# Layer 1's strips: their new rows and partial sums loaded from ScalarE's queue, not from SP's

## The chip, the cores and the metric

One NeuronCore of a Trainium2 chip runs the whole kernel. The metric is the device time of one execution in microseconds (us); lower is better. Twelve runs of the kernel before have a median of 2482.11 us, the lowest 2476.35, the highest 2493.36.

## What is computed

A graph network of two layers over 3327 nodes (padded to 3328 = 26 blocks of 128) with 128 features. Layer 0 is a four-headed graph attention; layer 1, in which the change lies, is a graph convolution. Both have a norm in front and add to their input:

```
h = max(layernorm(x), 0)
x = x + L0(h, adj)            # attention, 4 heads, concatenated, times w
h = max(layernorm(x), 0)
x = x + L1(h, adj)
def L1(H, A, W, b):
    A_t = A + I;  D = A_t.sum(axis=1);  D_inv = D ** -0.5
    return relu((D_inv[:, None] * A_t * D_inv[None, :]) @ (H @ W.T + b))
```

About 2% of the adjacency matrix is not zero.

## The kernel before

**Layer 0** goes over the 26 blocks of nodes. For each it gathers rows of neighbours from a table in HBM, scores and weighs them, and closes the block (`close`): from the aggregate `agn` come the new rows `xn` of `x` (L786), stored to `xn_d` (L788, by SP), and from `xn` a row of the norm: `agn` again (L793, L794 on ScalarE), a transpose (L798 on TensorE), its copy (L799), a product with `gwT` (L806), `L809` on VectorE, and at last `x_sb[:, b]` (L811 on ScalarE). After that `x_sb[:, b]` holds what layer 1 multiplies for block b, already scaled.

**Layer 1** needs, for each row of the output, the sum over all 26 columns of blocks of `x_sb[:, j]` times the adjacency. The output is made in seven *strips* of four blocks (the last has two), transposed: `strips[s, j]` is a 128x512 tile of the turned adjacency, kept in HBM as `AT_d`. Much of these sums is done while layer 0 still runs: columns that were closed early are summed in `prep` and stored as `part1_d` (one partial sum per block, none for strip 0); for strips 1, 2 and 3 twelve columns more are summed by `begin` and stored as `part2_d`. What is left are 74 products of a column and a strip, in this order (`work`): strip 0 columns 0 to 24, strip 1 columns 14 to 24, then column 25 of strips 0 and 1, then strip 2 (18 to 25), strip 3 (22 to 25), strip 4 (14 to 25), strip 5 (18 to 25), strip 6 (22 to 25). Each product is L1006, in fp32 two matmul instructions on the page. Numbered 0 to 73, the strips end with products 36, 37, 45, 49, 61, 69 and 73.

The tiles for the products come in seven *pieces* of 11 products (the last of 8). `strip` (L911) loads a piece into one of four buffers `g`, by DMAs that alternate between SP's queue and GpSimd's (L915, L916). Piece 4 holds products 44 to 54, piece 5 products 55 to 65, piece 6 products 66 to 73. A buffer comes free when the last product of the piece four before has run: piece 6 takes the buffer of piece 2, so it waits for product 32.

A strip ends in two steps:

- `strip_in(s)` (L955) takes tiles `r0` (three buffers) and `r1` (two) and issues up to three loads: `xn_d` rows into `r0[:, 0]` (L961), `part1_d` into `r1[:, 0]` (L963, not for strip 0), `part2_d` into `r0[:, 1]` (L965, strips 1, 2 and 3). Each is 256 KB (128 KB for strip 6). It is called at the first product of strips 0 and 1, and for the others at the fifth product of the strip or at its last, whichever comes first (L1003).
- `strip_out(s)` (L968) is a generator that the loop advances once per product. It starts after the strip's last product: VectorE adds `part2` (L973) and `part1` (L975) to the sum (strip 0, with neither, is copied by ScalarE, L977). Two advances later TensorE transposes it (L982, four at a time), VectorE adds `x_sb`, multiplies by `dinv`, takes the maximum and adds the new rows (L983, L984, L985), and ScalarE's queue stores the result (L986).

**What sets the order.** The whole is written by hand under a manual schedule: each engine runs its instructions in the order in which the loop records them, and waits where it must. TensorE's queue therefore holds the transposes of strip s (L982) some products after its end, and nothing behind them runs until they have; ScalarE's queue holds the instructions of `close` for block 25 among all else. While the first 36 products run, `close` of block 25 is spread between them: in TensorE's order its transpose L798 stands after product 29, and product 36 is the first that needs block 25's `x_sb`.

**Waits of a DMA.** In the built program the DMAs of SP and of ScalarE together take turns, in the order in which they were recorded, on eight completion semaphores (DMAHW0 to DMAHW7). A DMA waits, on the engine that issues it, until the DMA that had the same semaphore before it has landed.

Of the kernel before, what the change touches and what calls it, by code (L numbers as in the profile page):

```python
# [15 lines left out]
P = 128  # L16
# [215 lines left out]
def _sparse_layers(tc, nc, x, adj, w1, w2, a, wlin, w, gw, gb, gb_sb, gwT, x_sb, dinv, flag, ident, out):  # L232
# [24 lines left out]
    with ExitStack() as l0:  # L257
# [4 lines left out]
        xn_d = dram.tile([NP, D], F32, name="xn_d")  # L262
        part1_d = dram.tile([D, NP], F32, name="part1_d")
        part2_d = dram.tile([D, NP], F32, name="part2_d")
# [80 lines left out]
        def finished(b):  # L345

            return max(0, 4 * (b // 4) - 2)
# [607 lines left out]
        def strip_in(s):  # L955

            n = min(4, NB - 4 * s)
            r0 = pr.tile([P, 2, BANK], F32, name="r0", bufs=3).rearrange("p k (b d) -> p k b d", b=4)[:, :, :n]
            r1 = pr.tile([P, 2, BANK], F32, name="r1").rearrange("p k (b d) -> p k b d", b=4)[:, :, :n]
            rows = slice(4 * s * P, (4 * s + n) * P)  # L960
            nc.sync.dma_start(r0[:, 0], xn_d[rows, :].rearrange("(b p) d -> p b d", p=P))  # L961
            if finished(4 * s):
                nc.sync.dma_start(r1[:, 0], part1_d[:, rows].rearrange("p (b i) -> p b i", b=n))  # L963
            if s in early:
                nc.sync.dma_start(r0[:, 1], part2_d[:, rows].rearrange("p (b i) -> p b i", b=n))  # L965
            return n, rows, r0, r1

        def strip_out(s, po, n, rows, r0, r1):  # L968
# [26 lines left out]
        def layer1():  # L995
            ending, sums, ins = [], {}, {}
            for i, (s, j) in enumerate(work):
                if i == in_front:
                    yield "all"
                w = min(4, NB - 4 * s) * P  # L1000
                if s not in sums:
                    sums[s] = ps_z.tile([P, 2, BANK], F32, name="z")[:, 0]
                if j == min(NB - 1, first_column(s) + 4 * (s not in front)):  # L1003
                    assert len(ending) < 2
                    ins[s] = strip_in(s)
                nc.tensor.matmul(sums[s][:, :w], x_sb[:, j, :], strips[s, j][:, :w], start=(j == first_column(s)), stop=(j == NB - 1))  # L1006
                if i % PIECE == PIECE - 1 or i == len(work) - 1:
                    allow("g")
                ending[:] = [f for f in ending if next(f, "end") != "end"]
                if j == NB - 1:  # L1010
                    ending.append(strip_out(s, sums.pop(s), *ins.pop(s)))
                yield "one"
            for e in ending:
                for _ in e:
                    pass
# [194 lines left out]
        with tc.manual_schedule():  # L1210
# [4 lines left out]
            n = len(groups)  # L1215
# [8 lines left out]
            for i in range(-1, n + 1):  # L1224
                if i + 1 < n:
                    slot()
                if 0 <= i < n:
                    b, hb, m = groups[i]
# [153 lines left out]
```

## Time and profile before

| | |
|---|---|
| median of 12 runs | 2482.11 us (2476.35 to 2493.36) |
| the profiled execution | 2481.43 us |
| its span, first to last instruction of the program | 2479.3 us |
| share of the span, busy: TensorE, VectorE, ScalarE, GpSimd | 90%, 83%, 26%, 71% |
| mean busy share of the DMA engines, up to the last two slices of 40 | 90% or more in each slice |
| last product and scores of layer 0 on TensorE (L657) | 2384.69 to 2385.40 |
| the 74 products of layer 1 (L1006) | 2385.33 to 2469.45 |
| strip endings on TensorE (L982), strips 0 to 6, start | 2425.13, 2438.17, 2447.43, 2451.59, 2462.39, 2468.42, 2471.59 |
| last L985 on VectorE | 2472.99 to 2473.41 |

Of 2479.3 us the last 95 are layer 1's products and strip endings; all that the change touches runs after 2386. In the tables of the trace, times are us from the start of the span. PE is TensorE, DVE VectorE, ACT ScalarE, POOL GpSimd, SP SyncE; a "q" behind the name is the engine's sequencer, which issues DMAs and waits. A row of the timeline gives start, duration, engine, line, operation, the tiles written and read, their shape and how many instructions were merged; in brackets the engine's idle time before it and what ended it.

### The profile page before, as it was taken

How to read it: one execution, taken by the hardware profiler on the slowest of the kernel's cores; microseconds unless marked ns; L12 is line 12 of the kernel's file. 1: busy time of each engine (PE TensorE's matmuls, PEld its weight loads, DVE VectorE, ACT ScalarE, POOL GpSimd, SP SyncE). 2: the span in 40 equal slices, each digit the busy share in tenths (PEclk: the TensorE clock that was granted, in tenths of full speed). 3: DMA queues.
4: the chain of work that ended last, by engine and by line, in shares of the span. 5: the costliest groups of instructions: out<-in, count | busy, mean ns of one | idle time of the engine just before them, and what ended most of it. 6: DMA issues, size and time to landing. Idle time of an engine off the chain costs nothing.

```text
span 2479.3 us, 51942 instructions
## 1 busy us (share of the span) xinstructions
PE 2223.3 (90%) x19254; PEld 1594.2 (64%) x19254; DVE 2053.6 (83%) x6426; ACT 639.7 (26%) x1547; POOL 1765.9 (71%) x1867
## 2 busy tenths in 40 slices
PE   6589889988988998999999999899999999999996
PEld 4456666666666666666676676666667667666653
DVE  7688988898898898889888888988988988896633
ACT  4122222223222222322222222232222222221110
POOL 3577777777777777777777777777777777777750
PEclk8699999999999999999999999999999999999998
DMA  9999999999999999999999999999999999999996
GB/s 302 375 352 328 351 329 317 352 354 325 323 368 333 326 358 345 326 334 364 327 329 349 344 315 347 349 321 329 360 325 323 355 343 318 338 335 330 366 306 174
DMA packets 401715, 826.93 MB, mean 334 GB/s; under 512 B 38435, under 2 KB 270383, under 8 KB 398127
## 3 DMA queue, kind: packets, MB, share of 16 engines
q0 software_dynamic: 144464, 628.85, 72.2%
q1 hardware_dynamic: 165343, 147.87, 18.9%
q10 hardware_dynamic: 91648, 46.80, 6.3%
q8 instruction: 155, 2.54, 0.4%
q14 instruction: 105, 0.86, 0.1%
HBM read 754.47 MB, written 113.22 MB: 350 GB/s over the span
## 4 chain that ended last, share of the span: by engine, by line
PE 40%; DVE 26%; DMA 17%; POOL 9%; issue 6%; SPq 1%; ACT 1%; DVEq 0%; POOLq 0%; ACTq 0%
DVE r L638 14%; PE z L622 14%; DMA g<-table,idx 13%; PE s L657 10%; POOL g L595 9%; DVE cand L422 3%; PE ag L670 2%; PE z L627 2%; DVE codes L410 2%; PE tr L379 1%; DVE cand L456 1%; DVE lists L453 1%; PE tr L942 1%; PE z L1006 1%; PE z L1124 1%
## 5 line engine op out<-in xcount | busy, mean ns | idle before, releaser
L595 POOL DMA_INDIRECT g<-table,idx x1664 | 1611.5, 968 | 576.7 <-issue 418.8
L638 DVE TENSOR_TENSOR r<-z,x1n 128x1024 f32<-128x1024 f32 x832 | 1010.8, 1215 | 130.7 <-PE z L622 128.2
L622 PE MATMUL z<-ident,g 128*128 128x128 f32 x6656 | 922.5, 278 | 107.8 <-DVE r L638 97.3
L622 PEld LDWEIGHTS z<-ident,g 128*128 128x128 f32 x6656 | 750.9, 142 | 245.2 <-DVE r L638 145.8
L657 PE MATMUL s<-r,sel 128*4 128x512 f32 (+1 forms) x3744 | 504.9, 579 | 9.9 <-DVE r L638 9.5
L698 ACT COPY ssb<-s 128x512 f32<-128x512 f32 x208 | 122.0, 586 | 495.5 <-PE s L657 495.0
L657 PEld LDWEIGHTS s<-r,sel 128*4 128x4 f32 x3744 | 86.1, 85 | 254.5 <-issue 179.8
L422 DVE MAX8 cand<-codes 128x8 f32<-128x52 uint16 x1664 | 217.7, 206 | 0.0
L670 PEld LDWEIGHTS ag<-g,wt 128*32 128x32 f32 x3328 | 117.7, 110 | 101.2 <-issue 93.8
L670 PE MATMUL ag<-g,wt 128*32 128x133 f32 x3328 | 159.4, 278 | 0.0
L633 DVE TENSOR_TENSOR r<-z,x1n 128x128 f32<-128x128 f32 x104 | 30.1, 289 | 151.4 <-PE z L627 149.0
L730 ACT ACTIVATE sc<-sc 128x32 f32<-128x32 f32 x208 | 47.9, 230 | 414.4 <-DVE sc L725 252.1
L367 ACT COPY at<-tr 128x512 f32<-128x512 f32 (+1 forms) x175 | 97.1, 555 | 215.0 <-PE tr L365 203.8
L453 DVE MAX8 lists<-cand 128x8 f32<-128x272 f32 (+1 forms) x338 | 133.2, 394 | 2.2
L365 PE MATMUL tr<-ident,adjb 128*128 128x128 f32 x676 | 109.1, 285 | 26.0 <-DMA adjb<-in_adj_dram 16.5
L635 ACT ACTIVATE r<-z 128x512 f32<-128x512 f32 x104 | 62.1, 597 | 258.0 <-DVE r L633 258.0
L709 PE MATMUL tr<-ident,ssb 128*128 128x128 f32 x832 | 124.9, 273 | 2.1 <-ACT ssb L698 2.1
L627 PE MATMUL z<-oi,x1b 128*128 128x256 f32 x416 | 125.2, 383 | 0.0
L595 POOL DMA_INDIRECT ge<-table,idxo x104 | 99.2, 953 | 32.9 <-issue 14.0
L456 DVE MATCH_REPLACE8 cand<-lists,cand 128x272 f32<-128x272 f32 (+1 forms) x312 | 118.0, 378 | 0.0
L410 DVE SCALAR_TENSOR_TENSOR codes<-adjb,code 128x832 uint16<-128x832 f32 x104 | 104.2, 1018 | 12.8 <-DMA adjb<-in_adj_dram 12.8
L622 PE MATMUL z<-ident,ge 128*128 128x128 f32 x416 | 83.1, 282 | 26.6 <-DVE r L638 26.6
(200 smaller groups left out, 2444.1 us busy)
## 6 DMA issues: line engine op xcount, KB each, us to landing
adjb<-in_adj_dram SPq DMA_DIRECT2D x26, 1664.0 KB
table<-AT_d SPq DMA_DIRECT2D x26, 1664.0 KB
AT_d<-at ACTq DMA_DIRECT2D x150, 256.0 KB
g<-table,idx POOLq DMA_INDIRECT x1664
table<-img SPq DMA_DIRECT2D x12, 1296.0 KB
adjb<-AT_d SPq DMA_DIRECT2D x72, 128.0 KB
g<-AT_d SPq DMA_DIRECT2D x25, 256.0 KB
g<-AT_d POOLq DMA_DIRECT2D x25, 256.0 KB
```

Of the source, the lines that this page charges most:

```text
L410: nc.vector.scalar_tensor_tensor(codes[:, i], adjb[:, c0:c0 + part], 0.0, code[:, c0:c0 + part], op0=OP.not_equal, op1=OP.mult, accum_out= ...
L422: nc.vector.max(cand[:, c, 8:].rearrange("p (r s) -> p r s", s=32)[:, :, sgm % 32], codes.rearrange("p a b -> p (a b)")[:, sgm % 32 * SEG: ...
L453: nc.vector.max(top, of)
L456: nc.vector.match_replace(out=of, in_to_replace=top, in_values=of, imm_value=0.0)
L595: return nc.gpsimd.indirect_dma_start(out=g[:, t, lo:hi], out_offset=None, in_=tab, in_offset=bass.IndirectOffsetOnAxis(ap=at[:, t:t + 1], ...
L622: nc.tensor.matmul(z[:, i, q * P:(q + 1) * P], g[:, m % 2 * 4 + q, c0:c0 + D], ident, is_transpose=True, start=(q == 0 or m < 8), stop=(m ...
L627: nc.tensor.matmul(z[:, i, :n], k.x1b[:, h * D:(h + 1) * D], k.oi[:, hb * n:(hb + 1) * n], start=False, stop=True, skip_group_check=True)
L638: nc.vector.tensor_tensor(r.rearrange("p h (i s) -> p h i s", s=16), z.rearrange("p h (i s) -> p h i s", s=16), k.x1n[:, 2 * hp:2 * hp + 2 ...
L657: nc.tensor.matmul(k.s[32 * h:32 * h + 4, :n], sel[:, h, 31 - row:35 - row], r[h // 2][:, h % 2, :n], start=(row == 0), stop=(last and (m ...
L670: nc.tensor.matmul(k.ag[32 * cg:32 * cg + 32, u, :WORK], wt[:, t].rearrange("p h q -> p (h q)"), g[:, t, f0:f0 + WORK], start=(w == 0 and ...
L698: nc.scalar.copy(ssb, s)
L709: nc.tensor.transpose(pt[:, q, :], ssb[:, q * P:(q + 1) * P], ident)
```

## The change

Three calls in `strip_in` go from SP's queue to ScalarE's; nothing else is changed.

```diff
-            nc.sync.dma_start(r0[:, 0], xn_d[rows, :].rearrange("(b p) d -> p b d", p=P))
+            nc.scalar.dma_start(r0[:, 0], xn_d[rows, :].rearrange("(b p) d -> p b d", p=P))
             if finished(4 * s):
-                nc.sync.dma_start(r1[:, 0], part1_d[:, rows].rearrange("p (b i) -> p b i", b=n))
+                nc.scalar.dma_start(r1[:, 0], part1_d[:, rows].rearrange("p (b i) -> p b i", b=n))
             if s in early:
-                nc.sync.dma_start(r0[:, 1], part2_d[:, rows].rearrange("p (b i) -> p b i", b=n))
+                nc.scalar.dma_start(r0[:, 1], part2_d[:, rows].rearrange("p (b i) -> p b i", b=n))
```

Seven strips issue 7 + 6 + 3 = 16 DMAs. In the built programs the instructions of TensorE, VectorE and GpSimd stand in the same order as before; SP has the 16 fewer and ScalarE the 16 more. On ScalarE they stand so (the waits are those of the built program after the change; DMA names its destination and source):

```
L698 TensorCopy ssb<-s 128x512 [waits PE_49]
L961 DMACopy r_29158<-xn_d 128x4x128 [waits DMAHW7_49]
L730 Activation sc<-sc 128x44 [waits DVE_49,Activation_49]
...
L774 TensorCopy outT<-tr 128x512 [waits DMAHW2_49,PE_49]
L961 DMACopy r_29292<-xn_d 128x4x128 [waits DMAHW6_49]
L963 DMACopy r_29293<-part_d 128x512 [waits DMAHW0_49]
L965 DMACopy r_29292<-part_d 128x512 [waits DMAHW3_49]
L793 Activation agn<-xn,st 128x128 [waits DVE_49,Activation_49]
...
L986 DMACopy out_dram<-r_29158 128x4x128 [waits DMAHW1_49,DVE_49]
L986 DMACopy out_dram<-r_29292 128x4x128 [waits DMAHW2_49,DVE_49]
L961 DMACopy r_29379<-xn_d 128x4x128 [waits DMAHW3_49]
L963 DMACopy r_29380<-part_d 128x512 [waits DMAHW4_49]
L965 DMACopy r_29379<-part_d 128x512 [waits DMAHW5_49]
L986 DMACopy out_dram<-r_29379 128x4x128 [waits DMAHW6_49,DVE_49]
L961 DMACopy r_29403<-xn_d 128x4x128 [waits DMAHW1_49,DMAHW7_49,PE_49,Activation_49]
```

From there on it goes on in the same way: the store of strip s, then the loads of strip s + 1 (loads of strips 2, 3, 4, 5 and 6 behind the stores of strips 1, 2, 3, 4 and 5).

## The prediction

> **What bounds the kernel now.** The change acts in the last 95 us alone, so I read that stretch: first the timeline of TensorE, VectorE and SP, to see where the products stand still and for what.
>
> ```profile
> 2425.57 1.02 PE L1006 MATMUL z<-g,x_sb 128*128 128x512 f32 x2
> 2438.17 1.12 PE L982 MATMUL tr<-ident,r 128*128 128x128 f32 x4 [11.58 <-DVE r L975]
> 2439.08 8.51 PE L1006 MATMUL z<-g,x_sb 128*128 128x512 f32 x16
> 2447.86 3.60 PE L1006 MATMUL z<-g,x_sb 128*128 128x512 f32 x8
> ...
> 2436.70 0.69 DVE L973 TENSOR_TENSOR r<-z,r 128x512 f32<-128x512 f32 x1 [15.50 <-DMA r<-part_d]
> ...
> 2429.85 0.83 SPq L961 DMA_DIRECT2D r<-xn_d  x1
> 2431.02 0.48 SPq L963 DMA_DIRECT2D r<-part_d  x1
> 2431.56 0.42 SPq L965 DMA_DIRECT2D r<-part_d  x1
> ```
>
> TensorE is never idle for long but once: 11.58 us before strip 1's transposes, because strip 1's partial sums were issued only at 2431.56, behind the pieces in SP's queue. The stall costs more than itself: sixteen matmuls took 8.51 us after it, against 2 x 3.60 for the same number later, and its four transposes 1.12 against 0.60; the granted clock in the windows of 10 us says why (columns: length, busy time of PE, PEld, DVE, ACT and POOL, clock, DMA share, GB/s). That is 1.9 us more.
>
> ```profile
> 2420.00:2430.00 10.00, 6.51 (x19) 2.54 (x17) 0.52 (x3) 0.99 (x2) 1.16 (x2) 1.00 1.10 287
> 2430.00:2440.00 10.00, 1.83 (x6) 1.32 (x7) 3.20 (x5) 0.00 (x0) 0.00 (x0) 0.59 1.00 270
> ```
>
> Second, the chain of waits, for how long SP's loads of pieces take, with SP's own waits.
>
> ```profile
> 2412.30 1.97 SPq L916
> 2414.32 14.69 DMA g<-AT_d
> 2429.02 0.78 SPq L916
> 2431.56 5.05 DMA r<-part_d
> ...
> SPq L963 <- DVE r L985: 13.8, 3, 5.0
> SPq L961 <- DMA out_dram<-r: 11.1, 3, 4.6
> ```
>
> The load issued at 2414.32 (sixth of SP's eight for piece 4) landed at 2429.01, 14.7 us later, and a load eight places behind waited for it: the turn of the semaphores is a real wait. The DMA engines are full until about 2437 (share 1.10, then 1.00).
>
> Third, ScalarE, into whose queue the loads go.
>
> ```profile
> 2408.22 0.59 ACT L774 COPY outT<-tr 128x512 f32<-128x512 f32 x1 [2.24 <-PE tr L771]
> 2413.13 0.40 ACT L793 ACTIVATE agn<-xn,st 128x128 f32<-128x128 f32 x1 [4.32 <-DVE st L787]
> ...
> 2440.20 33.62 ACTq L986 DMA_DIRECT2D out_dram<-r  x7
> ```
>
> It has 4.3 us to spare before L793, and after 2423 only the seven stores. Its idle time looks like room for the loads; the question is what stands behind them.
>
> **The change, part by part.**
>
> *Strip 0's load* now stands before L730. Its semaphore's last user is SP's fourth load of piece 1, whose semaphore updates in the trace end at 2389.4; so L730, at 2387.52 before, comes at about 2389.4 + 0.4 = 2389.8, 2.3 late. What waits for it: L664 and L681 on VectorE, done at 2388.50 and 2390.45, read by TensorE at 2395.41 (L670) and 2397.82 (L690). Cover 6.9 and 7.4 us, cost 0; without it, 2.3. SP loses the 1.07 us of this issue at 2396.32.
>
> *Strip 1's three loads* now stand between L774 and L793. In the built program they share semaphores with SP's third, fifth and eighth load of piece 4. By the semaphore updates these landed at 2423.6, 2428.1 and 2429.4 (the chain's row for the sixth, 2429.01, lies between). So ScalarE, done with L774 at 2408.81, does not reach L793 at 2413.1 but after the eighth has landed. Some of that comes sooner: GpSimd's three loads of piece 6 (768 KB, issued from 2418.93 before) wait for product 32, which is now late, and no longer compete; strip 1's first load and about half of its second (400 KB) now do. (768 - 400) KB at 287 GB/s is 1.3 us, and SP's queue is one load lighter: I take 2427.4. With the issue of the last load (0.42) and 0.2 to start, L793 begins at 2428.0 instead of 2413.1. Bounds: 2424 if SP's queue, rid of a load and of the competition, drains 4 us earlier; 2431.6 if nothing is gained and both 256 KB loads (1.8 us) come first.
>
> Who waits for L793: TensorE's transpose L798, at 2415.78 before, and in its queue all products from number 30 on. L798 goes to 2428.0 + 0.45 = 2428.45. From L798 to the end of product 40 before: 2426.59 - 2415.78 = 10.8; plus 1.9, since TensorE has again been idle for 12 us. So strip 1's transposes start at 2441.2. The stall of 11.58 itself is gone: strip 1's loads, issued by 2427.8, land by 2433 even at the 5.05 us of the chain, and L973 asks for them at about 2438 (cover 5 us). Against 2438.17 that is **+3.0**: the stall has moved 25 products forward and grown.
>
> *What SP and GpSimd have behind:* piece 6's loads, at 2432.7 and 2418.9 before, now wait for product 32, at about 2431. They are read from product 66 on, after 2475: cover over 30 us, cost 0.
>
> *Strips 2 to 6.* Before, SP issued these loads while products ran, held at most by a buffer. Now each strip's loads stand behind the store of the strip before, which waits for its L985. That closes a ring from strip to strip: transposes 0.45, L983 to L985 2.2, issue of the store 0.45, issues of the loads 0.46 apart, landing, L973 and L975 (0.72 each), transposes again. Landing after issue: strip 3's part2, issued 2445.18, landed 2449.3, 4.1 us; strip 5's part1, issued 2454.59 beside a store, 4.2; strip 6's half-size load, issued 2465.20, 2.2 (2.5 with the store in front). From strip 1's transposes as zero, products at 0.865 each (half for strip 6's), start of L982 before and now:
>
> - strip 2: 9.3 before. TensorE could be there at 7.4; stores of strips 0 and 1 issue at 1.3 and 3.4, part2 is issued at 4.9 and lands at 9.0; two adds: 10.5. **+1.2**
> - strip 3: 4.1 later before (four products). Now 2.2 + 0.5 + 1.4 to part2's landing 4.1 on, and two adds: 9.7 later. **+5.5**
> - strip 4: 10.8 later in both; the loads land in time (28.0, sum done at 28.4). **0**
> - strip 5: 6.0 before; the ring with two loads and one add: 8.6. **+2.6**
> - strip 6: 3.2 before; the ring with half-size loads: 6.6. **+3.4**
> - last L985 after it: **+0.1**
>
> Together +12.8. TensorE's idle 5.8 us before strip 3 may halve the clock again, up to 1.9 before strip 4; I take +0.7. Bounds for all of these strips: landings of 2.2 (the shortest) make the sum +6.8, landings of 5.05 (the chain's, the longest) with the clock drop +18.
>
> Sum: 3.0 + 12.8 + 0.7 = **+16.5 us**. The profiled execution has 2479.3 + 2.1 outside its span = 2481.4; 0.7 more is the median. 2482.1 + 16.5 = 2498.6, **2498.5**.
>
> [...]
>
> **The rivals.**
>
> *ScalarE is not held (not slower).* Were SP's loads of piece 4 down by 2413, the DMAs would cost only their issues (1.3 us of a 4.3 us gap) and strip 1's transposes start at 2426.6 at full clock, 11.6 earlier. With strips 2 to 6 as above the end comes at 2426.6 + 35.2 + 12.8 + 0.7 = 2475.3 against 2473.4: +2, 2484; with landings of 2.2, -5. It decides from L793 later than about 2416. For it: ScalarE's spare time, and that SP's first loads of a piece land within 8 us. Against: 14.69 us in the chain, and the eighth load issued only at 2420.5.
>
> *The ring is hidden.* If loads land before the products of each strip are done, only the +3.0 stays: 2485. For it: before, none of these loads was waited for. Against: they were issued earlier; strip 3's now come 14 us after strip 1's transposes, when TensorE needs them at once.
>
> *ScalarE is held longer and each landing is slow.* L793 at 2431.6, landings of 5.05, both clock drops: +6.6 + 18 = 2506.7. For it: three queues share the DMA engines until 2437. Against: afterwards the DMA share falls (0.69 and less).
>
> *The change isn't what it says:* excluded; the sixteen DMAs stand on ScalarE's queue in the built program.
>
> **How the numbers follow.** Forecast 0.77 (2490 to 2504); not held 0.08 (2477 to 2486); ring hidden 0.08 (2484 to 2490); slowest 0.07 (2504 to 2510). The range holds the forecast and half of its neighbours: **2490 to 2505**. A measurement can tell 0.2%, 5 us, from no change. Faster than that: 0.03, part of the first rival. Within: the rest of it and half of the second, 0.09. Slower: 0.88.
>
> **What would show it.** In the profile after: L793 at 2426 to 2430 with idle time of about 17 us before it, or an issue of L965 just ahead; TensorE idle some 12 us before L798 and not before strip 1's L982; idle times before L982 of strips 2, 3, 5 and 6 that end with r loads, about 3, 6, 3 and 5 us; L961 of each strip right behind a store. If L793 still starts near 2413, or L982 of strip 3 follows strip 2's within 5 us, the corresponding term is wrong.

## The result and the profile after

| | before | after |
|---|---|---|
| median, lowest to highest | 2483.02 us, 2476.35 to 2493.36 (50 runs) | 2502.25 us, 2495.94 to 2507.64 (12 runs) |
| ratio of the runs | | 1.0075, 95% interval 1.0065 to 1.0085 |
| the profiled execution, its span | 2481.43, 2479.3 | 2502.66, 2500.5 |
| first product L1006 starts | 2385.33 | 2387.87 |
| last L985 ends, after the first product | 88.08 | 106.87 |

The change makes the kernel 19.2 us slower; 2498.5 was predicted, 2490 to 2505 as its range. The last stage alone is 106.87 - 88.08 = 18.8 us longer. From here on a place in this stage is given as its distance from the first product (us), so that executions can be laid over each other whatever layer 0 took. The end of the stage means the end of the last L985.

TensorE's timeline after the change (start, duration, what ran, in brackets the idle time before it and what ended it):

```profile
2414.89 3.60 PE L1006 MATMUL z<-g,x_sb 128*128 128x512 f32 x8
2430.26 0.47 PE L798 MATMUL tr<-ident,agn 128*128 128x128 f32 x1 [11.77 <-ACT agn L793]
2430.53 6.96 PE L1006 MATMUL z<-g,x_sb 128*128 128x512 f32 x10
...
2443.56 0.60 PE L982 MATMUL tr<-ident,r 128*128 128x128 f32 x4
2444.00 7.03 PE L1006 MATMUL z<-g,x_sb 128*128 128x512 f32 x16
2454.47 0.63 PE L982 MATMUL tr<-ident,r 128*128 128x128 f32 x4 [3.44 <-DVE r L975]
2454.94 3.60 PE L1006 MATMUL z<-g,x_sb 128*128 128x512 f32 x8
2464.34 1.12 PE L982 MATMUL tr<-ident,r 128*128 128x128 f32 x4 [5.80 <-DVE r L975]
2465.25 12.67 PE L1006 MATMUL z<-g,x_sb 128*128 128x512 f32 x24
...
2485.73 0.66 PE L982 MATMUL tr<-ident,r 128*128 128x128 f32 x4 [1.78 <-DVE r L975]
...
2492.68 0.69 PE L982 MATMUL tr<-ident,r 128*128 128x128 f32 x2 [5.86 <-DVE r L975]
```

The long stall of before, 11.58 us ahead of strip 1's transposes (now at 2443.56, without a bracket), is gone. In its place stand 11.77 us ahead of L798, in block 25, three new ones ahead of strips 2, 3 and 5, and the one ahead of strip 6 has grown from 2.14 to 5.86 us. ScalarE's timeline says where the first comes from:

```profile
2410.76 0.59 ACT L774 COPY outT<-tr 128x512 f32<-128x512 f32 x1 [2.24 <-DMA g<-AT_d]
2422.12 0.37 ACTq L961 DMA_DIRECT2D r<-xn_d  x1
2427.11 0.34 ACTq L963 DMA_DIRECT2D r<-part_d  x1
2429.36 0.34 ACTq L965 DMA_DIRECT2D r<-part_d  x1
2429.80 0.40 ACT L793 ACTIVATE agn<-xn,st 128x128 f32<-128x128 f32 x1 [18.46 <-DMA r<-xn_d]
...
2445.07 2.45 ACTq L986 DMA_DIRECT2D out_dram<-r  x2
2447.56 0.52 ACTq L961 DMA_DIRECT2D r<-xn_d  x1
```

The three loads of strip 1 take 0.34 to 0.37 us each to issue, but stand at 2422.12, 2427.11 and 2429.36: each waits for its turn of a semaphore. By the semaphore updates in the trace, SP's loads of piece 4 that had the same three semaphores before them landed at 2422.10, 2427.08 and 2429.34, each within 0.03 us of the issue that waited. L793, which wants nothing from these loads, waits 18.46 us behind them. Further down, strip 2's first load (2447.56) follows directly on the stores of strips 0 and 1. Its semaphore was free long before, at 2434.75, so there it is the place behind the stores that holds it. The chain of waits confirms both. It names the transfer that ScalarE's queue waited for last (part of a piece of the adjacency, which SP issued), and then the ring from strip to strip:

```profile
2421.59 7.75 DMA g<-AT_d
2429.36 0.34 ACTq L965
...
2429.80 0.41 ACT agn L793
2430.26 0.47 PE tr L798
...
2458.90 3.84 DMA r<-part_d
...
2462.86 0.70 DVE r L973
```

The clock, in the windows of 10 us (length, busy time of PE, PEld, DVE, ACT and POOL, clock, DMA share, GB/s): the idle stretch has moved from 2430 to 2420, and a second dip has come ahead of strip 4.

```profile
2420.00:2430.00 10.00, 0.00 (x0) 0.00 (x0) 0.00 (x0) 0.20 (x1) 0.00 (x0) 0.59 1.12 289
...
2460.00:2470.00 10.00, 5.66 (x10) 2.87 (x11) 3.46 (x5) 0.00 (x0) 0.00 (x0) 0.66 0.32 94
```

### The profile page after: what moved, and what is told of

It reads as the page before. It is cut to its first block, busy times and chain, and to the rows that moved or that the text cites. A ratio compares the mean times of both kernels' runs of the same rounds, so it can differ in the third digit from the quotient of the medians.

```text
span 2500.5 us, 51935 instructions
## 1 busy us (share of the span) xinstructions
PE 2230.3 (89%) x19254; PEld 1595.6 (64%) x19254; DVE 2054.3 (82%) x6426; ACT 639.7 (26%) x1547; POOL 1770.9 (71%) x1867
## 4 chain that ended last, share of the span: by engine, by line
PE 41%; DVE 26%; DMA 16%; POOL 10%; issue 6%; SPq 1%; ACT 1%; ACTq 0%; DVEq 0%; POOLq 0%
PE z L622 15%; DVE r L638 14%; DMA g<-table,idx 12%; PE s L657 10%; POOL g L595 10%; DVE cand L422 3%; PE ag L670 2%; PE z L627 2%; DVE codes L410 1%; DVE cand L456 1%; PE tr L379 1%; PE z L1006 1%; DVE lists L453 1%; PE tr L942 1%; PE z L1124 1%
## 5 line engine op out<-in xcount | busy, mean ns | idle before, releaser
L670 PEld LDWEIGHTS ag<-g,wt 128*32 128x32 f32 x3328 | 117.2, 110 | 102.5 <-issue 95.3
L670 PE MATMUL ag<-g,wt 128*32 128x133 f32 x3328 | 159.1, 278 | 0.0
L730 ACT ACTIVATE sc<-sc 128x32 f32<-128x32 f32 x208 | 47.9, 230 | 414.3 <-DVE sc L725 252.6
```

Source lines behind the costliest of these rows:

```text
L670: nc.tensor.matmul(k.ag[32 * cg:32 * cg + 32, u, :WORK], wt[:, t].rearrange("p h q -> p (h q)"), g[:, t, f0:f0 + WORK], start=(w == 0 and ...
```

## The experiments

The kernels ran on several chips. On two of them every kernel takes some 900 to 1,100 us longer, before included (3377.36 and 3568.25 us). That lies in layer 0: the first product starts only at 3263 to 3470 us there. Their last stage runs at the usual lengths, so the table of places below holds for all, while a ratio from them has a wide interval. Each row of places is one profiled execution. Where a kernel was profiled twice, the ends of its stage differ by 0.6 us (before), 4.3 (after), 1.3 and 4.6 (own tiles), so a difference of a few us between two rows shows little by itself.

| kernel | L793 starts | strip 1's L982 | last L985 ends | ratio, 95% interval |
|---|---|---|---|---|
| before | 27.80 | 52.84 | 88.08 | |
| before, once more | 27.80 | 52.54 | 88.69 | |
| after | 41.93 | 55.69 | 106.87 | 1.0075 (1.0065 to 1.0085) |
| after, once more | 42.02 | 54.67 | 102.53 | 1.0074 (1.0060 to 1.0088) |
| strips 0, 1 from ScalarE | 40.19 | 53.37 | 87.87 | 1.0007 (0.9986 to 1.0028) |
| strips 2 to 6 from ScalarE | 27.79 | 50.45 | 101.75 | 1.0051 (1.0020 to 1.0083) |
| after, stores from SP | 40.80 | 53.73 | 88.03 | 1.0007 (0.9982 to 1.0032) |
| strips 0, 1 early, SP | 27.79 | 41.10 | 82.54 | 0.9994 (0.9974 to 1.0014) |
| strips 0, 1 early, ScalarE | 27.80 | 41.10 | 82.77 | 0.9983 (0.9964 to 1.0002) |
| strips 0, 1 early, GpSimd | 27.79 | 41.09 | 87.02 | 0.9997 (0.9988 to 1.0007) |
| own tiles, strips 0 to 2 from GpSimd | 27.79 | 41.09 | 81.86 | 0.9979 (0.9968 to 0.9991) |
| the same once more | 27.79 | 41.10 | 80.61 | 0.9964 (0.9946 to 0.9982) |
| own tiles, strips 0 to 3 from GpSimd | 27.80 | 41.09 | 74.38 | 0.9961 (0.9941 to 0.9980) |
| the same once more | 27.79 | 41.09 | 78.96 | 0.9948 (0.9931 to 0.9965) |

### Both kernels once more

> The kernel before, once more with a trace, as the measure of the last stage on the chip of the three runs beside it. From the first product to the last L985 about 88 us; if the stage itself differs from chip to chip by more than 3 us, stages of other chips can't be set side by side.

> The kernel after, timed and traced on the same chip: the last stage 17 to 20 us longer than in the kernel before, in the same places (L798, L982 of strips 2, 3, 5, 6).

Before: 2487.31 us in its profiled run. After: 2499.49 against a median of 2481.62. The stalls of after are in the same places (11.86 us before L798, then 3.06, 3.68, 1.83 and 5.92), but the stage ends at 102.53 against 88.69: +13.8 in this pair of executions, less than the 17 to 20 expected, and +18.8 in the first pair. Most of the 5 us between the pairs is the clock: 2.6 us is a clock drop ahead of strip 4 in the first after (granted 0.66 between 2460 and 2470) that the second does not repeat, and 0.9 us more is a longer stretch of slow matmuls in the second before (the sixteen after strip 1 took 9.44 us, not 8.51). Of the differences between the profiled times, 21.2 and 16.4 us, 2.5 and 3.0 us lie ahead of the first product. TensorE's timeline in the second profile of after, with its clock drop ahead of strip 3 (granted 0.68 between 2460 and 2465, 1.00 between 2465 and 2470):

```profile
2458.97 0.63 PE L982 MATMUL tr<-ident,r 128*128 128x128 f32 x4 [3.06 <-DVE r L975]
2459.44 5.30 PE L1006 MATMUL z<-g,x_sb 128*128 128x512 f32 x8
2468.41 0.66 PE L982 MATMUL tr<-ident,r 128*128 128x128 f32 x4 [3.68 <-DVE r L975]
2468.91 10.47 PE L1006 MATMUL z<-g,x_sb 128*128 128x512 f32 x24
```

### One half of the change: the loads of strips 0 and 1

```diff
+            eng = nc.scalar if s < 2 else nc.sync
-            nc.sync.dma_start(r0[:, 0], ...
+            eng.dma_start(r0[:, 0], ...
```

(So too for the other two loads. The edit adds a line, so what is L975, L982 or L1006 above stands a line lower in its trace: the transposes are L983.)

> Only the loads of strips 0 and 1 from ScalarE, those of strips 2 to 6 from SP. Theory of two costs (ScalarE held before L793; a ring of store and loads at strips 2 to 6): the hold alone. L793 still about 16 us late, the idle time of about 12 us on TensorE still before L798, but strips 3, 5 and 6 wait for no load; the time is 1 to 4 us over before. Rival, the hold does it all: 19 us over before, as with the whole change. Rival, ScalarE's queue is slow for any load: well over 4 us, with strip 1's loads landing late and TensorE waiting at strip 1's L982.

```profile
3303.59 0.48 PE L798 MATMUL tr<-ident,agn 128*128 128x128 f32 x1 [10.02 <-ACT agn L793]
...
3316.32 0.60 PE L983 MATMUL tr<-ident,r 128*128 128x128 f32 x4
3316.76 7.03 PE L1007 MATMUL z<-g,x_sb 128*128 128x512 f32 x16
3324.01 0.63 PE L983 MATMUL tr<-ident,r 128*128 128x128 f32 x4 [0.23 <-DVE r L976]
...
3328.76 0.66 PE L983 MATMUL tr<-ident,r 128*128 128x128 f32 x4 [0.68 <-DVE r L976]
```

L793 starts at 40.19, 12.4 us late (about 16 were expected), behind the same three loads, and strip 1's transposes at 53.37 instead of 52.84. The sixteen matmuls after them take 7.03 us, not 8.51: the slow ones now lie ahead of strip 1, where the ten behind L798 take 6.38 us (4.46 in before). Strips 2 to 6, loaded by SP, lose little, and the stage ends at 87.87. This half alone moves the stall and is neutral, to within the interval of its ratio (-5 to +9 us); 1 to 4 us over before were expected.

### The other half: the loads of strips 2 to 6

```diff
+            eng = nc.sync if s < 2 else nc.scalar
```

> Only the loads of strips 2 to 6 from ScalarE, those of strips 0 and 1 from SP. Theory of two costs: the ring alone. L793 as before at its 28 us after the first product, the 11.6 us before strip 1's L982 as before, then idle times before L982 of strips 2, 3, 5 and 6 of about 2, 6, 2 and 6 us: 13 to 17 us over before, so that e1 and e2 add up to the whole change. Rival, the hold does it all: no change.

TensorE's timeline (line numbers as in the first half):

```profile
3334.48 1.12 PE L983 MATMUL tr<-ident,r 128*128 128x128 f32 x4 [9.19 <-DVE r L976]
...
3346.07 0.64 PE L983 MATMUL tr<-ident,r 128*128 128x128 f32 x4 [1.59 <-DVE r L976]
...
3356.04 1.12 PE L983 MATMUL tr<-ident,r 128*128 128x128 f32 x4 [5.90 <-DVE r L976]
```

L793 is on time, the old stall ahead of strip 1 stands (9.19 us, where 11.6 were expected), and the new ones ahead of strips 2 and 3 (1.59, 5.90), 5 and 6 (1.82, 5.85) are there as in after. The stage ends at 101.75, 13.7 us over before, within the 13 to 17 expected: this half holds most of the loss. From strip 1's transposes to the end it takes 51.3 us, after 51.2 (47.9 in its second profile), before 35.2. The ends of the two halves add up to -0.2 + 13.7 = +13.5 us, which is the +13.8 of the second pair of profiles but not the +18.8 of the first; the ratios, 1.0007 and 1.0051 against 1.0075, agree within their intervals.

### The stores taken out of the ring

After, with L986 on SP's queue, so that no load stands behind a store.

```diff
-            nc.scalar.dma_start(out[rows, :].rearrange("(b p) d -> p b d", p=P), xo)
+            nc.sync.dma_start(out[rows, :].rearrange("(b p) d -> p b d", p=P), xo)
```

> The whole change, and the seven stores of the output (L986) from SP's queue: loads and stores have changed queues. Theory: the ring is broken, since no load stands behind a store; the hold before L793 stays: 1 to 4 us over before, like e1. Rival, a load from ScalarE's queue is itself slower or the queues disturb each other: still 15 to 20 us over before.

```profile
3341.87 0.47 PE L798 MATMUL tr<-ident,agn 128*128 128x128 f32 x1 [10.64 <-ACT agn L793]
...
3361.83 0.63 PE L982 MATMUL tr<-ident,r 128*128 128x128 f32 x4
...
3366.82 0.66 PE L982 MATMUL tr<-ident,r 128*128 128x128 f32 x4 [0.93 <-DVE r L975]
```

All sixteen loads still go from ScalarE's queue, and block 25 is held as in after (10.64 us); but strip 2 has no bracket, strip 3 waits 0.93, and from strip 1's transposes to the end it takes 34.3 us, not 51.2. The stage ends at 88.03, where before ends at 88.08 (1 to 4 us over were expected). So it is the store ahead of the loads, not ScalarE's queue, that costs strips 2 to 6 their time.

### Where the loads stand, and which queue issues them

Three kernels call `strip_in` for strips 0 and 1 at product 0, instead of at products 0 and 25; the other strips stay with SP. They differ in the queue of these four loads alone: SP, ScalarE, GpSimd.

```diff
-                if j == min(NB - 1, first_column(s) + 4 * (s not in front)):
-                    assert len(ending) < 2
-                    ins[s] = strip_in(s)
+                for t in front if i == 0 else () if s in front else (s,):
+                    if i == 0 or j == min(NB - 1, first_column(s) + 4):
+                        ins[t] = strip_in(t)
```

> The kernel before, with strip 1's three loads called at product 0, next to strip 0's, still from SP. Theory, the stall of 11.6 us comes only from the loads' place in SP's order: TensorE no longer waits at strip 1's L982. But strip 2's loads are still behind pieces 5 and 6 and land at about 2442, so part of the idle time goes to strip 2's L982: 2 to 5 us under before. Rival, the DMA engines are full and the order does not matter: no change, with the idle time of about 11 us in another place.

> Strips 0 and 1 are loaded from ScalarE's queue, both at the stage's start (ahead of L730), strips 2 to 6 from SP as before. Theory (ScalarE's queue costs only through the compute that stands behind a load that waits for its turn): at the start nothing of the last stage stands behind the six loads but L730 and the evictions of block 24, which have some 7 us of cover; L793 ends at about 27.8 us after the stage's first product as before, strip 1's stall of 11.6 us goes, and the stage ends about 82 to 84 us after its first product, against 88.1 before: 2 to 6 us faster. Rival (DMA issue on ScalarE's queue holds its evictions wherever it stands): L793 comes late by several us, or TensorE idles at L670 or L690 in front of block 24, and the time is that of before or more.

> The kernel before with the loads of strips 0 and 1 called at product 0 and issued from GpSimd, which waits for a buffer there for some 7 us; strips 2 to 6 as before, from SP. Theory: no wait before L798 or strip 1's L982; strip 2's loads are still behind SP's pieces 5 and 6, so some 5 us of idle time stay before strip 2's L982, as in e4: 4 to 7 us under before. Rival, GpSimd's queue is slower to bring them: TensorE waits again at strip 1's L982, no gain.

ScalarE's timeline of the second (its loads are L962, L964 and L966):

```profile
3467.48 1.30 ACTq L962 DMA_DIRECT2D r<-xn_d  x2
3469.72 0.34 ACTq L964 DMA_DIRECT2D r<-part_d  x1
3470.34 0.47 ACTq L966 DMA_DIRECT2D r<-part_d  x1
3470.91 0.24 ACT L730 ACTIVATE sc<-sc 128x44 f32<-128x44 f32 x1 [2.85 <-DMA g<-AT_d]
...
3495.15 0.40 ACT L793 ACTIVATE agn<-xn,st 128x128 f32<-128x128 f32 x1 [4.32 <-DVE st L787]
```

The same four loads (the expectation's six is a slip) on ScalarE's queue, ahead of L730: L730 comes 1.4 us later than before (3.55 us after the first product, not 2.19), L793 has its old 4.32 us of slack back and starts on time, and no product waits. The stage ends at 82.77, with the loads on SP at the same place at 82.54. At one place the choice between SP and ScalarE makes 0.2 us; the place in the queue makes 5.1 us on ScalarE (87.87 with strip 1's loads at product 25, 82.77 at product 0) and 5.5 us on SP (88.08 and 82.54).

In the time of the kernel none of the three gains anything that can be measured, for each interval holds 1 (2 to 5, 2 to 6 and 4 to 7 us were expected). Strip 1's stall goes, and a part of it comes back ahead of strip 2 (5.6 us with SP and ScalarE). With GpSimd's queue nearly all of it does; TensorE's timeline:

```profile
2429.03 0.60 PE L983 MATMUL tr<-ident,r 128*128 128x128 f32 x4
...
2447.63 1.08 PE L983 MATMUL tr<-ident,r 128*128 128x128 f32 x4 [11.13 <-DVE r L976]
```

Strip 2's loads stay with SP, behind its pieces. With strips 0 and 1 on GpSimd's queue, SP's loads of pieces last to 46.8 us after the first product, with them on SP to 42.8; so the third load of strip 2 is issued at 51.2 (2439.14) instead of 47.2, and lands 6.9 us later. The gain of 4 to 7 us that was expected is lost there. What keeps SP 4 us longer wasn't taken apart.

### Tiles of their own, and the loads spread

Strips wait for tiles `r0` and `r1` too, so loads can't be called at will. Two kernels give each strip's loads their own space (`r0`, `r1` and an adjacency tile that is free by then), load part1 and part2 first, compute in place and call the loads early. Of their edit, shortened, with comments added here:

```diff
+            eng = nc.gpsimd if s < 3 else nc.sync        # second kernel: s < 4
...
+                for t in {0: (0, 1), 24: (2,), 34: (3, 4), 36: (5, 6)}.get(i, ()):
+                # second kernel: {0: (0, 1), 24: (2,), 28: (3,), 34: (4,), 36: (5, 6)}
+                    ins[t] = strip_in(t)
```

> The kernel before with tiles of their own for every strip's loads (the buffers r0 and r1, and the tile adjb, which is free by then), so that none waits for a buffer: strips 0 and 1 at product 0 and strip 2 at product 24 from GpSimd, strips 3 to 6 at products 34 and 36 from SP behind piece 6. Theory: all waits before L982 are gone but for what the full DMA engines leave (at most 5 us, at strip 2 or 3), and the clock is not halved: 8 to 13 us under before. Rival, the DMA engines bind until about 52 us after the first product whatever the order: the idle time only moves, no more gain than e7.

> The kernel with tiles of their own for each strip's loads once more, beside the two others on the same chip: 0.9979 of before within 0.0012, with TensorE idle 5 to 6 us in front of strip 3's transposes.

> As the kernel with tiles of their own for each strip's loads, but strip 3's loads too go from GpSimd's queue, at product 28, ahead of piece 6; strip 4's at 34 and 5's and 6's at 36 from SP. Theory (order in the queues is what costs): strip 3's wait of 5.95 us goes, with the halved clock behind it, and the stage ends about 75 to 79 us after its first product: 8 to 12 us faster than before. Rival (the DMA engines are full up to about 59 us after the first product, so an earlier load only displaces a piece): the wait moves to a piece of the adjacency or to strip 4, and the time is that of the kernel whose strip 3 goes from SP, 5 to 7 us faster than before.

> The kernel whose strips 0 to 3 are loaded from GpSimd's queue into tiles of their own, once more, for its size where layer 0 takes less of the time. Theory: TensorE is idle nowhere between the first product and strip 6's transposes, the stage ends 74.4 us after its first product where before takes 88.1 to 88.7, and the kernel is 13 to 15 us faster than before. Rival (the end of the program waits for something else than the strips): the stage is as short, but the time falls by less than 10 us.

The first measured 2475.75 us against 2481.62 (0.9979), 5.9 us faster where 8 to 13 were expected. TensorE (the transposes are L997 here, the products L1021) runs through strip 2 and then waits 5.95 us for strip 3's loads (3.96 in the repeat, where 5 to 6 were expected), with a lower clock behind it (granted 0.82 between 2445 and 2455; before took 10.46 us for the same 24 matmuls):

```profile
2445.24 1.11 PE L997 MATMUL tr<-ident,adjb 128*128 128x128 f32 x4 [5.95 <-DVE adjb L990]
2446.14 11.72 PE L1021 MATMUL z<-g,x_sb 128*128 128x512 f32 x24
```

The second takes that wait away: in its first profile TensorE is idle nowhere up to strip 6's transposes and the stage ends at 74.38 (75 to 79 expected). In its repeat the stage ends at 78.96, and TensorE's timeline has a new wait, for a piece of the adjacency:

```profile
2423.30 4.46 PE L1021 MATMUL z<-g,x_sb 128*128 128x512 f32 x10
2430.42 4.51 PE L1021 MATMUL z<-g,x_sb 128*128 128x512 f32 x6 [2.66 <-DMA g<-AT_d]
2434.76 0.60 PE L997 MATMUL tr<-ident,r 128*128 128x128 f32 x4
```

There the rival may be right in part: the DMA engines are full (share 1.04 between 2422 and 2432), though no run here shows that it was one of the strips' loads that delayed this piece. The time of this repeat, on a chip of the usual speed, is **2469.31 us against 2483.08, ratio 0.9948 (0.9931 to 0.9965)**: the lowest of all, and faster than both kernels of this study. That its gain of 13.8 us meets the 13 to 15 expected is partly luck, for the stage did not come as expected: it is only 9.1 and 9.7 us shorter than in the two profiles of before. Most of the rest lies ahead of the first product, which starts at 2381.77 (2385.33 and 2390.80 in before), and isn't explained. Nor is the second kernel shown to be faster than the first: on the one chip where both were timed the ratios are 0.9961 and 0.9964.

## Why the prediction was right

The direction, the places of the stalls and their causes came as forecast, and the size (+16.5 us) lies between the two pairs of profiles (+13.8 and +18.8). By the steps of its sum, each measured from the one before it (after less before, in the two profiled executions):

| step | predicted | measured | how |
|---|---|---|---|
| L793 (before: 2413.1) | 2428.0 | 2427.26 | 41.93 after the first product, put on the clock of before |
| L798 | 2428.45 | 2427.72 | 42.39 after it |
| strip 1's L982 | +3.0 | +2.85 | 55.69 - 52.84 |
| strip 2 | +1.2 | +1.65 | 66.60 - 62.10 = 4.50 |
| strip 3 | +5.5 | +5.7 | 76.47 - 66.26 = 10.21 |
| strip 4, clock in front of it | 0 + 0.7 | +2.6 | 89.89 - 77.06 = 12.83 |
| strip 5 | +2.6 | +1.9 | 97.86 - 83.09 = 14.77 |
| strip 6 | +3.4 | +3.8 | 104.81 - 86.26 = 18.55 |
| last L985 | +0.1 | +0.25 | 106.87 - 88.08 = 18.79 |
| sum | +16.5 | +18.8 | |

*The hold.* L793 waits behind strip 1's loads for SP's piece 4, and the turn of the semaphores does it, as the landings at 2422.10, 2427.08 and 2429.34 show. The same loads ahead of L730, where the turns come round sooner (the last issue ends 3.45 us after the first product, not 41.83), hold L730 by 1.4 us and no product (L793 at 27.80). The rival in which ScalarE isn't held asked for L793 before about 2416; it started 18.46 us after ScalarE was done. That strip 1's step comes so near, +2.85 for +3.0, is partly luck: L793 was 0.7 us earlier than forecast, and from L798 to strip 1's transposes it took 13.30 us, not 12.7. The ten matmuls behind the pause took 6.96 us against 4.46 (granted clock 0.50 from 2430 to 2435, 0.72 between 2435 and 2436, then 1.00), so the clock cost 2.5 us there, where 1.9 was taken.

*The ring.* The stalls ahead of strips 2, 3, 5 and 6 were given as about 3, 6, 3 and 5 us; they are 3.44, 5.80, 1.78 and 5.86. With the stores elsewhere they shrink to nothing, 0.93, nothing and the 2.14 that before has too. The rival of the hidden ring falls with that, and the slowest one with the landings: part2 of strips 2 and 3 landed 4.03 and 3.84 us after issue (4.1 taken), strip 5's part1 3.24 (4.2 taken, which is why strip 5 came out too dear), strip 6's 2.52 (2.5).

*Costs put at nothing.* L730 was 1.2 us late (2.3 forecast), and TensorE's L670 and L690 show no idle time before them. Piece 6 was held for 16.30 us by product 32, as foreseen, and no product that reads it waited for more than 0.2.

*The term that was mis-sized* is the clock drop before strip 4: taken at +0.7 of a possible 1.9, it came in full and a little above. The 24 matmuls after strip 3's transposes took 12.67 us against 10.46 (granted clock 0.50 from 2463 to 2469), 2.2 more; with strip 4's own remainder that is 1.9 of the 2.3 us by which the sum is short. In the second profile of after the drop comes one strip sooner (eight matmuls in 5.30 us against 3.60, 1.7 more), where TensorE has to wait for strip 3's loads anyway, and not again (10.47). With that pair the stage is 13.8 us longer, less than the +16.5 of the sum, so the +18.8 is one draw, not the size to the last us.

*A sum that was not made* is that of each half alone. The first half, with its 12 us of hold, is neutral by itself (87.87 against 88.08): it only trades one stall for another, and gets back a part of what the slow matmuls ahead of strip 1 cost (6.38 us, not 4.46) behind it (7.03, not 8.51). Nearly all of the loss belongs to strips 2 to 6 (16 us of the 18.8 lie behind strip 1's transposes), and there to a store.

*What stays open:* the 2.5 and 3.0 us ahead of the first product, in layer 0, which the change doesn't touch. It starts at 2387.87 and 2393.77 in after, and between 2381.77 and 2390.80 in the five profiles of before (two) and of variants of it (three) on chips of this speed. These overlap, and no run settles whether there is an effect.

## What to carry to other kernels

Moving a DMA to an idle-looking engine moved its wait too (here L793 stood 18.46 us behind three loads that take 0.34 to 0.37 us each to issue): look up which instruction stands behind it in that engine's queue and who needs that, and what stands ahead of it. A load behind a store that waits for the result before it closed a ring from one step to the next (51.2 us from strip 1's transposes to the end, 34.3 with the stores on another queue); put the two on different queues. Issuing the loads earlier, into space of their own, gained more here (2469.31 us against 2483.08) than any choice of queue, which gained nothing that could be measured. Those kernels also changed the order of the loads and took GpSimd's queue for some, and what each of these is worth wasn't taken apart.

## What the hardware showed that was not expected

Whether a short pause costs the clock can't be read from its length alone. An idle time of 3.44 us (after, strip 2) left the next eight matmuls at 3.60 us (granted clock 1.00 in each window of 1 us from 2452 to 2459), one of 3.06 us in its second profile made them 5.30, and one of 2.66 us in the fastest kernel gave six matmuls in 4.51 (0.53 between 2432 and 2434). The granted clock of that second profile of after, in windows of 1 us, with the columns as above:

```profile
2457.00:2458.00 1.00, 0.00 (x0) 0.00 (x0) 0.59 (x1) 0.00 (x0) 0.00 (x0) 1.00 0.00 0
...
2459.00:2460.00 1.00, 1.00 (x6) 0.70 (x7) 0.36 (x1) 0.00 (x0) 0.00 (x0) 0.90 0.00 0
2460.00:2461.00 1.00, 1.00 (x3) 0.48 (x2) 0.97 (x2) 0.00 (x0) 0.00 (x0) 0.50 0.00 0
...
2463.00:2464.00 1.00, 1.00 (x3) 0.38 (x2) 0.00 (x0) 0.00 (x0) 0.00 (x0) 0.90 0.96 230
2464.00:2465.00 1.00, 0.73 (x2) 0.00 (x0) 0.00 (x0) 0.00 (x0) 0.00 (x0) 1.00 1.03 314
```

TensorE pauses until 2458.97 at full clock (1.00 in the windows up to 2459); the clock halves after the work has begun again, at about 2459.8, and is back at about 2463.2 (both from the windows with 0.90, which hold 0.2 us of half clock each): 3.4 us.

Behind the longer pause of 5.80 us, ahead of strip 3 in the first profile of after, the order is the other one: the clock is 0.93 between 2462 and 2463, 0.50 from 2463 to 2469 and 0.66 between 2469 and 2470. So it is down before the transposes at 2464.34, and stays down for about 6.8 us. What decides when such a drop begins and how long it lasts, no run shows.
